# Moving four small steps of a perceiver block's main loop: context sums ahead of the router's shares on GpSimd, logits behind the third quarter's product, choice behind the next norm's moments

## The chip, the cores and the metric

The kernel runs on one core of a Trainium2 chip. The metric is the device time in microseconds (us) of one execution; the figure of a kernel is the median of its timed runs. Engines are called by their names: TensorE (PE in the profile, PEld for its weight loads), VectorE (DVE), ScalarE (ACT), GpSimd (POOL) and SyncE (SP), which issues most of the DMAs.

## The reference, cut to what matters

One block is computed for 16 batches of x (128 tokens x 512 features, float32), each with a context of 2048 x 512:

```
x = x + xattn(layernorm(x), ctx)     # softmax(h ctx^T) ctx, no projections
x = x + attn(layernorm(x))           # 16 heads of 32, rotary on half of each, causal
x = x + ffn(layernorm(x))            # 2 of 8 experts, rank 64
```

The last step is the one whose small parts the change moves. For a batch, the logits are the first token of the normed x times Wr^T (8 x 512). The two largest are kept, their softmax gives two gates, and the residual gets h + sum over both of gate x (h A_e^T) B_e^T:

```
logits = cls_tok @ Wr.T
top_vals, top_idx = jax.lax.top_k(logits, 2)
...
weighted = jnp.einsum('be,belh->blh', gates, expert_out)
return x + weighted
```

## The kernel before, in words

**Stages and order.** All three steps of all batches are in one program, unrolled. The main loop (L1008 to L1122) runs b from 0 to 13. A turn works on several batches at once: b is in its self-attention, l = b - 1 in its expert step, a = b + 1 in its cross-attention product, and s = b + 2 in its cross-attention scores; s + 1 has its first norm prepared. Batches 14 and 15 end in a tail written out by hand (from L1124). There is no planner: the order on every engine is the order of the calls, since each engine is wrapped so that its instructions keep program order (`InOrder`, L95 to L103). An engine therefore executes its list strictly in this order, and an instruction whose input isn't ready holds everything behind it on that engine. All instructions are issued through one helper line, L101, so the profile's rows are told apart by tiles.

**The cross-attention product.** The context of a batch comes in four quarters of 512 rows (`cts[a, v]`), and `attend(a, v, parts)` multiplies the exponentiated scores by quarter v on TensorE. For batches 2 to 14 the products are made with fewer multiplications from sums and differences of halves: `context_halves(a, v)` makes four sums of a context quarter on GpSimd (L344 to L354; tiles `more` and `ctx`), and `token_halves(a)` (L356) makes those of the scores, on VectorE and GpSimd (tile `blocks`). A quarter's product has a first part (8 records in the trace) and a second one (20 records). The first part of quarter 3 reads the last of the four context sums. In the loop the first parts of quarters 0 to 2 come early, then the second parts of 0, 1 and 2 at L1046, L1055 and L1063, and quarter 3 whole at L1078.

**Self-attention of batch b.** `powers(b, g)` (L597) makes a group of four heads: per head a masked scale with a running maximum on VectorE and an exponential on ScalarE. `divided(b, g)` divides a group, on GpSimd for g = 0 to 2, on ScalarE for g = 3. `sums(a)` (L319) adds up the softmax denominators of batch a in one VectorE reduction (tile `part`). `values_begun`, `values_moved`, `values_joined` put the values of b together on VectorE and ScalarE (tiles `vmoved`, `vfirst`, `vv`).

**The router of batch l.** `turn(3, l)` transposes the third norm's rows on VectorE and sends them through DRAM by two SyncE DMAs (`d`, then `hT`). `shares(l)` (L719) multiplies the first token's features by Wr on GpSimd (tile `g_share`), and a VectorE reduction leaves eight partial sums per partition (`g_part`). `logit(l)` (L730) sums these over the partitions with two products by ones on TensorE (`lg`; four records). `choose(l)` (L736) is five VectorE instructions (copy `g_z`, maxima, indices, a cast to `g_at`), one on GpSimd (`g_blocks`) and one on ScalarE. `fetch(l)` gathers the chosen experts' weights with three indirect DMAs from GpSimd (`each` twice, `wb` once) with two small index operations between. `residual(l)` adds the normed rows to x on GpSimd. Later `pair(l)` (L875) copies the gathered `each` on ScalarE for `middle(l)`'s products.

**The next first norm.** `norm1(s + 1)` (L256) is two VectorE instructions (`st`, `mv`) followed by three small ones on GpSimd (`rs` twice, `sh`).

**Space.** The accumulation banks are shared in turn. `logit` takes a bank of the two-deep pool that the scores `psc` use too, and gives it back when `choose` has copied it.

Of the kernel before, what the change touches and what calls it, by code (L numbers as in the profile page):

```python
# [20 lines left out]
B, S, V, D = 16, 128, 2048, 512  # L21
# [45 lines left out]
def perceiver_block(ctx: ExitStack, tc: tile.TileContext, io: dict, out: bass.AP):  # L67
# [38 lines left out]
    def bank(of, tag, name):  # L106
        return of.tile([P, 512], F32, tag=tag, name=name)
# [4 lines left out]
    def early(b):  # L112
        return b < 2

    def late(b):
        return b >= B - 2
# [139 lines left out]
    def norm1(b):  # L256
        norms[1, b] = Norm(xs[b], f"1_{b}", mixed=early(b), hT=(p2, "hT1"), by_act=b > 2).moments()
# [58 lines left out]
    def power(b, v):  # L316
        act.activation(scs[b][:, v], scs[b][:, v], AF.Exp)

    def sums(b, by=dve):  # L319
        sc = scs[b]  # L320
        part = p1.tile([P, S], F32, tag="part", name=f"part_{b}")
        parts[b] = part
        if by_halves(b):
            of = halves_of[b]
            dve.tensor_reduce(
                part.rearrange("p (m t) -> p m t", m=2),
                of[:, :2].rearrange("p m v k t -> p m t (v k)"), AX.X, ALU.add,
            )
            return
        t = p1.tile([P, 4, S], F32, tag="first", name=f"sums_{b}")  # L330
        for v in range(1, VC):
            by.tensor_tensor(t, sc[:, v], t if v > 1 else sc[:, 0], ALU.add)
        by.tensor_tensor(t[:, :2], t[:, :2], t[:, 2:], ALU.add)
        by.tensor_tensor(part, t[:, 0], t[:, 1], ALU.add)
# [6 lines left out]
    def by_halves(b):  # L341
        return 1 < b < B - 1

    def feature_halves(of, more, by=pool):  # L344
        b11, b12, b21, b22 = (of[:, 2 * k : 2 * k + 2, n * HD : (n + 1) * HD] for k in (0, 1) for n in (0, 1))
        by.tensor_tensor(more[:, 1], b22, b12, ALU.subtract)
        by.tensor_tensor(b12, b12, b11, ALU.subtract)
        by.tensor_tensor(more[:, 0], b22, b12, ALU.subtract)
        by.tensor_tensor(more[:, 2], b21, more[:, 0], ALU.subtract)

    def context_halves(b, v):
        if by_halves(b):
            mores[b, v] = p4.tile([P, 3, 2, HD], F32, tag="more", name=f"more_{b}_{v}")
            feature_halves(cts[b, v], mores[b, v])  # L354
# [145 lines left out]
    def order_tokens(b, copy=pool.tensor_copy):  # L500
        hTvs[b] = p1.tile([P, KC, S], F32, tag="hTv", name=f"hTv_{b}")
        copy(
            hTvs[b].rearrange("p c (i b) -> p c i b", i=Q),
            hTs[2, b].rearrange("p i c b -> p c i b"),
        )
# [67 lines left out]
    def values_joined(b):  # L573
        one, two, first, moved = state.pop(("v", b))
        values[b] = p1.tile([P, D], F32, tag="vv", name=f"vv_{b}")
        dve.tensor_tensor(values[b].rearrange("p (n d) -> p n d", n=2), two, first, ALU.add)
# [20 lines left out]
    def powers(b, g):  # L597
        att, nmx, sm, rsm, pss = atts[b]
        hs = slice(4 * g, 4 * g + 4)
        for i in range(hs.start, hs.stop):  # L600

            dve.tensor_tensor_reduce(
                att[:, i, :], pss[g][:, (i - 4 * g) * S : (i - 4 * g + 1) * S],
                cst[:, C_MASK : C_MASK + S], -SCALE, -NEG, ALU.add, ALU.min, nmx[:, i : i + 1],
            )
            act.activation(
                att[:, i, :], att[:, i, :], AF.Exp,
                bias=nmx[:, i : i + 1], scale=-1.0, accum_out=sm[:, i : i + 1],
            )

    def divided(b, g, by=pool):
        att, nmx, sm, rsm, pss = atts[b]
        hs = slice(4 * g, 4 * g + 4)
        dve.reciprocal(rsm[:, hs], sm[:, hs])
        if by is act:
            for i in range(hs.start, hs.stop):
                act.activation(att[:, i, :], att[:, i, :], AF.Copy, scale=rsm[:, i : i + 1])
            return
        by.tensor_tensor(
            att[:, hs, :], att[:, hs, :], rsm[:, hs, None].to_broadcast([P, 4, S]), ALU.mult  # L620
        )
# [92 lines left out]
    def small(b, n, tag, dtype=F32):  # L714
        return p2.tile([P, n], dtype, tag=f"g_{tag}", name=f"g_{tag}_{b}")

    parts_of, logits, chosen = {}, {}, {}

    def shares(b):  # L719
        share, part = small(b, E * KC, "share"), small(b, E, "part")  # L720
        share = share.rearrange("p (e c) -> p e c", e=E)
        first = hTs[3, b][:, 0, :, 0]
        (dve if late(b) else pool).tensor_tensor(
            share, w["r"].rearrange("p c e -> p e c"),
            first[:, None, :].to_broadcast([P, E, KC]), ALU.mult,
        )
        dve.tensor_reduce(part, share, AX.X, ALU.add)
        parts_of[b] = part

    def logit(b):  # L730
        logits[b] = bank(*((ps_acc, "acc") if b >= B - 3 else (ps_sc, "sc")), f"lg_{b}")
        part = parts_of.pop(b)
        for at in (slice(0, P // 2), slice(P // 2, P)):
            matmul(logits[b][at, :E], ones[:, at], part, start=True, stop=True)
# [273 lines left out]
    for b in range(B - 2):  # L1008
        l, a, s = b - 1, b + 1, b + 2
        if b:  # L1010
            order_tokens(b, act.copy)
            value_tokens(b)
            turn_max(a)
            most(a)
            x2_of(l)
        project(b, "q", [0, 1])
        if b:
            spread(a)
            for v in range(VC):
                less(a, v)  # L1020
                power(a, v)
            load_x(s + 1)
        if b:
            rows(3, l)
        project(b, "q", [2, 3])
        rotate(b, "q")
        project(b, "k")
        rotate(b, "k")
        if b:
            turn(3, l)  # L1030
            load_turned(s, 3)
        if b:
            values_by_halves(b)
        else:
            project_v(b)
            keep_v(b)
        rotated(b, "q")
        rotated(b, "k")
        attend(a, 0, (0,))
        attend(a, 1, (0,))  # L1040
        compare(b)
        attend(a, 2, (0,))
        if by_halves(a):
            token_halves(a)
        powers(b, 0)
        attend(a, 0, (1,))  # L1046
        powers(b, 1)
        if b:
            shares(l)
        context_halves(a, 3)  # L1050
        powers(b, 2)
        if b:
            values_begun(b)
        divided(b, 0)
        attend(a, 1, (1,))  # L1055
        powers(b, 3)
        if b:
            values_moved(b)
            logit(l)
        divided(b, 1)  # L1060
        load_ctx(a + 1, 0)
        load_ctx(a + 1, 1)
        attend(a, 2, (1,))  # L1063
        load_ctx(a + 1, 2)
        divided(b, 2)
        if b:
            sums(a)
            values_joined(b)
        divided(b, 3, act)
        if b:  # L1070
            choose(l)
            fetch(l)
            residual(l)
        if s + 1 < B:
            norm1(s + 1)
        if b == 0:
            value_weights()
        attend(a, 3)  # L1078
        load_ctx(a + 1, 3)
        whole(a)  # L1080
        attended(a)
        turn_probs(b, 0)
        if b:
            gate(l)
        begin_join(a)
        turn_probs(b, 1)
        joined(a)
        portion(a)
        x1_of(a)
        score(s, 0)  # L1090
        load_turned(s + 1, 0)
        keep_score(s, 0)
        turn_probs(b, 2)
        if b:
            pair(l)
        rows(2, a)
        score(s, 1)
        load_turned(s + 1, 1)
        keep_score(s, 1)
        turn(2, a)  # L1100
        turn_probs(b, 3)
        if s + 1 < B:
            rows(1, s + 1)
            turn(1, s + 1)
        context_halves(a + 1, 0)
        context_halves(a + 1, 1)
        score(s, 2)
        load_turned(s + 1, 2)
        if b:
            middle(l)  # L1110
        keep_score(s, 2)
        score(s, 3)
        if b:
            heads(b)
            widen(l)
            end(l)
            keep_heads(b)
        else:
            heads_by_halves(b)
        context_halves(a + 1, 2)  # L1120
        keep_score(s, 3)
        join(b)  # L1122

    y, z = B - 2, B - 1  # L1124
    l = y - 1
# [22 lines left out]
    powers(y, 1)  # L1148
    residual(l)
    shares(l)  # L1150
    sums(z, pool)
    powers(y, 2)
    attend(z, 2)
# [70 lines left out]
    end(l)  # L1224
    join_half(z, 0, [0, 1, 2])
    shares(y)
    logit(y)
    join_half(z, 0, [3])
    join_half(z, 1)
# [71 lines left out]
```

## Time and profile before

| what | value |
|---|---|
| median of the 3 timed runs | 769.77 us (768.87 to 770.97) |
| the profiled execution, its own time | 768.3 us |
| its span, first to last instruction | 766.5 us |
| granted TensorE clock over the span | 1.000 |
| TensorE busy | 759.1 us, 99% |
| VectorE busy | 615.0 us, 80% |
| GpSimd busy | 547.5 us, 71% |
| ScalarE busy | 321.5 us, 42% |
| DMA, mean over the span | 237 GB/s |

How to read the lines that follow. A line of the timeline has the start in us from the span's beginning, the duration in us, the engine, the operation with what it writes and reads, how many such in a row it stands for, and in brackets how long the engine was idle before and what ended that. A line of the chain that ended last has a start, a duration, an engine and what it wrote. Busy shares are means over the whole span; matmuls are pipelined, so a start says more than an end. Each turn of the main loop begins, in this text, with the first products of q.

### The profile page before, as it was taken

What the parts mean: (1) busy time and instruction counts of PE and PEld (TensorE: products, weight loads), DVE (VectorE), ACT (ScalarE), POOL (GpSimd) and SP (SyncE); (2) the same over time, 40 slices, a digit from 0 to 9 for tenths busy, and PEclk for the clock granted to TensorE, in tenths of its full rate; (3) what the DMA queues carried; (4) which work ended last, traced back from release to release, by engine and by line L of the source; (5) the groups of instructions that cost most, each with busy time, mean ns of one, the idle gap of its engine ahead of it and who ended that gap; (6) DMA issues with size and microseconds to landing.
All of it is one profiled execution on the core that took longest, in us unless ns stands there. A gap on an engine that the chain in (4) does not pass through costs nothing.

```text
span 766.5 us, 17831 instructions
## 1 busy us (share of the span) xinstructions
PE 759.1 (99%) x6752; PEld 602.3 (79%) x6752; DVE 615.0 (80%) x1678; ACT 321.5 (42%) x947; POOL 547.5 (71%) x604
## 2 busy tenths in 40 slices
PE   9999999999999999999999999999999999999997
PEld 9947587978778797887879788787978868797566
DVE  2447569899898988989899897989989898996466
ACT  1322426335363533535353354535435453442451
POOL 2002577888979888897988888788888979754633
PEclk9999999999999999999999999999999999999999
DMA  9989865759486584947657594765849567461003
GB/s 365 413 308 418 289 234 207 284 182 352 146 307 238 198 312 162 349 164 284 244 210 295 173 343 186 278 235 197 322 151 344 208 250 252 174 233 56 18 13 97
DMA packets 58229, 181.85 MB, mean 237 GB/s; under 512 B 5536, under 2 KB 27696, under 8 KB 41760
## 3 DMA queue, kind: packets, MB, share of 16 engines
q1 hardware_dynamic: 54048, 168.64, 60.0%
q0 software_dynamic: 3952, 12.02, 4.2%
q8 instruction: 53, 0.87, 0.4%
q14 instruction: 32, 0.26, 0.1%
q10 hardware_dynamic: 144, 0.07, 0.0%
HBM read 165.50 MB, written 15.20 MB: 236 GB/s over the span
## 4 chain that ended last, share of the span: by engine, by line
PE 94%; DVE 3%; POOL 1%; ACT 1%; issue 1%; DMA 0%; POOLq 0%
PE psc L101 30%; PE av L101 25%; PE q L101 7%; PE k L101 7%; PE o L101 7%; PE v L101 6%; PE pss L101 2%; PE y L101 2%; PE ffn L101 2%; PE mid L101 2%; PE fill L101 1%; ACT att L101 1%; DVE x L101 1%; PE den L101 1%; POOL more L101 0%
## 5 line engine op out<-in xcount | busy, mean ns | idle before, releaser
L101 PE MATMUL psc<-hT,ctxT 128*128 128x128 f32 x2048 | 233.9, 275 | 0.2 <-ACT hT L101 0.2
L101 PEld LDWEIGHTS psc<-hT,ctxT 128*128 128x128 f32 x2048 | 231.9, 192 | 0.8 <-ACT hT L101 0.4
L101 PE MATMUL av<-ctx,sc 128*64 128x256 f32 (+1 forms) x512 | 144.3, 422 | 0.0
L101 POOL TENSOR_TENSOR more<-ctx 128x512 f32<-128x512 f32 x104 | 132.8, 1277 | 4.4
L101 ACT ACTIVATE att<-att,nmx 128x128 f32<-128x128 f32 x256 | 98.9, 387 | 39.8 <-DVE nmx L101 39.8
L101 PEld LDWEIGHTS av<-ctx,sc 128*64 128x64 f32 (+1 forms) x512 | 72.4, 147 | 46.3 <-issue 19.4
L101 DVE STREAM_TRANSPOSE pT<-att 32x512 f32<-32x512 f32 x140 | 98.2, 701 | 3.8 <-POOL att L101 0.8
L101 PE MATMUL av<-ctx,blocks 128*64 128x256 f32 x416 | 97.1, 380 | 0.0
L101 PE MATMUL av<-more,sc 128*64 128x256 f32 x416 | 82.9, 381 | 0.3 <-POOL more L101 0.3
L101 POOL TENSOR_SCALAR rs<-mv 128x1 f32<-128x1 f32 x48 | 11.1, 232 | 84.2 <-DVE mv L101 82.0
L101 POOL TENSOR_TENSOR more<-ctx,more 128x512 f32<-128x512 f32 x52 | 66.3, 1276 | 4.1
L101 POOL TENSOR_TENSOR ctx<-ctx 128x512 f32<-128x512 f32 x52 | 66.3, 1275 | 4.1
L101 ACT ACTIVATE sc<-sc 128x512 f32<-128x512 f32 x64 | 38.5, 630 | 70.1 <-DVE sc L101 70.1
L101 PEld LDWEIGHTS av<-ctx,blocks 128*64 128x64 f32 x416 | 55.1, 137 | 14.8
L101 PEld LDWEIGHTS q<-hT,w_q 128*128 128x128 f32 x512 | 59.5, 192 | 4.1 <-issue 4.0
L101 PE MATMUL q<-hT,w_q 128*128 128x128 f32 x512 | 61.5, 275 | 0.0
L101 DVE CUSTOM_DVE_ANT_0 att<-pss,cst 128x128 f32<-128x128 f32 x256 | 57.2, 283 | 5.1 <-PE pss L101 4.7
L101 PE MATMUL k<-hT,w_k 128*128 128x128 f32 x512 | 59.8, 275 | 0.0
L101 PEld LDWEIGHTS k<-hT,w_k 128*128 128x128 f32 x512 | 58.5, 192 | 0.0
L101 PE MATMUL o<-w_c,yT 128*128 128x512 f32 (+1 forms) x136 | 58.4, 570 | 0.1
L101 POOL TENSOR_TENSOR att<-att,rsm 128x512 f32<-128x512 f32 x47 | 47.8, 1041 | 12.8 <-DVE rsm L101 12.8
L101 ACT COPY sc<-psc 128x512 f32<-128x512 f32 x64 | 37.2, 581 | 47.0 <-PE psc L101 47.0
(192 smaller groups left out, 1444.2 us busy)
## 6 DMA issues: line engine op xcount, KB each, us to landing
ctxT<-in_ctxT_dram SPq DMA_DIRECT2D x64, 1024.0 KB, 6.7
ctx<-in_ctx_dram SPq DMA_DIRECT2D x64, 1024.0 KB, 7.1
d<-turn SPq DMA_DIRECT2D x42, 256.0 KB, 3.0
hT<-d SPq DMA_DIRECT2D x42, 256.0 KB, 2.8
x<-in_x_dram SPq DMA_DIRECT2D x16, 256.0 KB, 6.1
out_dram<-x POOLq DMA_DIRECT2D x13, 256.0 KB, 6.0
down_q<-in_Wq_downT_dram SPq DMA_DIRECT2D x2, 1024.0 KB, 12.1
down_k<-in_Wk_downT_dram SPq DMA_DIRECT2D x2, 1024.0 KB, 9.9
```

The source lines that it names most:

```text
L101: return lambda *args, **kwargs: tc.keep_in_program_order(issue(*args, **kwargs))
```

## The change

Four calls move within the turn of the loop, and one function is cut in two so that its second half can move by itself.

1. `context_halves(a, 3)` goes in front of `shares(l)` (both have work on GpSimd).
2. `shares` loses its VectorE reduction, which becomes `share_sums`; in the loop that is called behind `sums(a)`. In the tail it directly follows `shares`, as before.
3. `logit(l)` goes from behind `values_moved(b)`, in front of the second part of quarter 2, to behind `values_joined(b)`; on TensorE it then stands between quarter 2's second part and quarter 3.
4. `norm1(s + 1)` goes in front of `choose(l)`, `fetch(l)` and `residual(l)`.

No operation is added or taken away, and no DMA changes its size or queue.

```
@@ shares
+        parts_of[b] = share, part
+
+    def share_sums(b):
+        share, part = parts_of[b]
         dve.tensor_reduce(part, share, AX.X, ALU.add)
         parts_of[b] = part
@@ the loop
         powers(b, 1)
+        context_halves(a, 3)
         if b:
             shares(l)
-        context_halves(a, 3)
         powers(b, 2)
...
             values_moved(b)
-            logit(l)
         divided(b, 1)
...
             sums(a)
+            share_sums(l)
             values_joined(b)
+            logit(l)
         divided(b, 3, act)
+        if s + 1 < B:
+            norm1(s + 1)
         if b:
             choose(l)
             fetch(l)
             residual(l)
-        if s + 1 < B:
-            norm1(s + 1)
@@ the tail, twice
     shares(l)
+    share_sums(l)
```

More of the change, by code (lines that the diff above doesn't have):

```diff
@@ L726, in shares, with share_sums @@
         )
+        parts_of[b] = share, part
+    def share_sums(b):
+        share, part = parts_of[b]
         dve.tensor_reduce(part, share, AX.X, ALU.add)
@@ L1047, in perceiver_block @@
         powers(b, 1)
+        context_halves(a, 3)
         if b:
             shares(l)
-        context_halves(a, 3)
         powers(b, 2)
@@ L1058, in perceiver_block @@
             values_moved(b)
-            logit(l)
         divided(b, 1)
@@ L1067, in perceiver_block @@
             sums(a)
+            share_sums(l)
             values_joined(b)
+            logit(l)
         divided(b, 3, act)
+        if s + 1 < B:
+            norm1(s + 1)
         if b:
@@ L1073, in perceiver_block @@
             residual(l)
-        if s + 1 < B:
-            norm1(s + 1)
         if b == 0:
@@ L1150, in perceiver_block @@
     shares(l)
+    share_sums(l)
     sums(z, pool)
@@ L1226, in perceiver_block @@
     shares(y)
+    share_sums(y)
     logit(y)
```

## The prediction

> **What bounds the kernel now.** I read the page's first part and its chain, then the waits of TensorE, then one steady turn of the main loop, engine by engine, from the timeline.
>
> ```profile
> PE 759.1 (99%) x6752; PEld 602.3 (79%) x6752; DVE 615.0 (80%) x1678; ACT 321.5 (42%) x947; POOL 547.5 (71%) x604
> ...
> PE 94%; DVE 3%; POOL 1%; ACT 1%; issue 1%; DMA 0%; POOLq 0%
> ```
>
> TensorE is busy 99% of the span and carries 94% of the chain that ends last. So nothing that another engine gains is worth anything unless TensorE waits for it, and every wait that TensorE gets is paid in full. The chain in order of time gives the length of a turn, from the first q products of one to those of the next:
>
> ```profile
> 200.32 1.79 PE q L101 x16
> ...
> 246.24 1.79 PE q L101 x16
> ...
> 291.18 1.79 PE q L101 x16
> ```
>
> 246.24 to 291.18 is 44.94 us, and eight of the turns b=2 to 13 take that. Four take more, by the same rows of the chain: b=3 (200.32 to 246.24) 45.92, b=6 45.01, b=9 45.46, b=12 45.35. Together they are 1.98 us above 4 x 44.94. Why is seen in b=3:
>
> ```profile
> 216.30 0.29 POOL L101 TENSOR_TENSOR g_share<-w_r,hT 128x32 f32<-128x32 f32 x1 [2.96 <-DMA hT<-d]
> ...
> 220.62 1.27 POOL L101 TENSOR_TENSOR more<-ctx,more 128x512 f32<-128x512 f32 x1
> ...
> 221.95 0.43 PE L101 MATMUL av<-more,sc 128*64 128x256 f32 x1 [0.34 <-POOL more L101]
> ```
>
> GpSimd stood 2.96 us waiting for the turned norm (hT) that the shares need; the four context operations queued behind the shares came late, and TensorE waited for them. In an ordinary turn (b=4) the same wait is 1.30 us and the last context operation ends at 264.89 + 1.28 = 266.17, before the last quarter's product begins at 266.94 (below).
>
> **Edit 1: context_halves(a, 3) ahead of shares.** Nothing is added. GpSimd's last operation before it ends at 259.26 (257.55 + 1.71, below), so the four operations, 1.35 apart, no longer sit behind the transfer. They end near 265.0 (below), in late turns as well, where they ended at 221.89 with TensorE due some 0.9 us earlier. The stalls of b=3, 6, 9 and 12 go: **-1.98 us**, if nothing is late next. The shares then run at 265.0 to 265.3; in b=4's time scale the latest transfer (b=3) landed at 262.2, so it is covered by 2.8 us.
>
> VectorE and GpSimd do hinder each other here:
>
> ```profile
> 257.55 1.71 POOL L101 TENSOR_TENSOR blocks<-blocks 128x512 f32<-128x512 f32 x1 [0.69 <-DVE blocks L101]
> ...
> 258.05 1.76 DVE L101 TENSOR_TENSOR blocks<-blocks,sc 128x512 f32<-128x512 f32 x1
> ```
>
> VectorE's instruction takes 1.76 where its neighbours of the same size (256.71, 257.44) take 0.70 and 0.69. It ends at 259.81, so it began to work at 259.12, just as GpSimd's 1.71 operation let go. Before, GpSimd then stood idle; now it has a context operation ready. Does that go first? The nearest row: in b=12 a VectorE cast started at 629.18 and took 0.19 (0.17 unhindered) between two of three queued GpSimd multiplications (627.29, 3.05 for three). VectorE got in between. I take no loss for VectorE, and 0.4 us for the first context operation, as the 1.71 row shows (1.28 unhindered): 259.66 + 4 x 1.35 = 265.0. The other end is one whole operation, 1.35 us, on VectorE's path: a rival below.
>
> [...] By "the queue goes first" the sum would be some 17.6 us worse (13 x 1.35); the b=12 cast says no.
>
> **Edit 2: the shares' reduction behind sums(a).** Per turn one 0.17 us VectorE instruction moves. Its old place gave a slot of 0.10 us (261.42 to 261.52 below), so all behind it until sums(a) is 0.10 earlier.
>
> **Edit 3: logit behind the third quarter's product and values_joined.** The products themselves cost the same at either place (0.09 us). But logit needs the reduction, and VectorE reaches that only after sums(a):
>
> ```profile
> 261.42 0.17 DVE L101 TENSOR_REDUCE g_part<-g_share 128x8 f32<-128x32 f32 x1
> ...
> 265.15 1.97 DVE L101 TENSOR_REDUCE part<-blocks 128x128 f32<-128x1024 f32 x1
> ...
> 264.66 0.24 PE L101 MATMUL lg<-g_part,ones 128*64 128x8 f32 x4
> 264.75 0.41 PE L101 MATMUL av<-ctx,sc 128*64 128x256 f32 x1
> ...
> 266.94 0.38 PE L101 MATMUL av<-ctx,sc 128*64 128x256 f32 x1
> ```
>
> The third quarter's second part has 20 records at 0.108: from 264.75 it reaches the last quarter at 266.94. With the 0.09 of lg gone from in front, TensorE comes to logit at 266.85. VectorE: sums end 267.12 - 0.10 = 267.02; an instruction that waits for nothing starts some 0.08 before its forerunner's end (the tail's 746.38 starts 0.09 before 746.28 + 0.19), so 266.94, + 0.17 = 267.11. TensorE reacts 0.05 later (722.15 + 0.76 = 722.91 to its load at 722.96): 267.16. From the load of a logit that had to wait to the next product the tail shows 0.14 (746.77 to 746.91): 267.30 or .31. Before, the last quarter began at 266.94. **The new wait is 0.37 us in each of 13 turns (b=1 to 13): +4.8 us.** TensorE's queue is in order; behind the logit stands the whole last quarter and all after it.
>
> Does VectorE run ahead over time? No: at 253.54 it stood 1.38 us waiting for TensorE's k products, so every turn starts from TensorE, and the distance from k to the reduction is fixed. Bounds: 0.28 (no reaction time, and 0.04 less on VectorE) to 0.65 (the 0.10 slot not gained, and the tail's other logit, which took 0.12 from reduction to load, 751.77 to 751.88, and 0.25 from load to next product). I take 0.37, worked from the nearest rows. The bank that the logit holds longer is next written in score(s, 1), at 273.9; the copy of z at about 269.0 frees it with 4.9 us to spare.
>
> **Edit 4: choose, fetch and residual behind norm1's moments.** On VectorE, two instructions (0.68 + 0.18, 0.86 with their gaps) now stand in front of the choice, whose five end at 269.18 in b=4 and will end near 270.0. On GpSimd the three root operations (0.24, 0.57, 0.26; 275.94 to 277.20 today) go in front of the block numbers, which move from 269.30 to 270.3. Three gathers (each of 1.09, 0.95 and 0.97 to issue), two index operations and the residual follow, all 0.95 later; in turn the roots no longer stand behind them, so GpSimd reaches the next root (277.97, after 0.77 idle) no later. No SP transfer moves. Who waits for the gathers:
>
> ```profile
> 277.51 0.62 ACT L101 COPY paired<-each 128x512 f32<-128x512 f32 x1 [2.87 <-DMA each<-in_A_dram,g_blocks]
> ...
> 279.25 0.81 ACT L101 ACTIVATE h<-x,sh,rs 128x512 f32<-128x512 f32 x1 [1.11 <-POOL sh L101]
> ```
>
> ScalarE's copy waits 2.87 for the gathers, then 1.11 for GpSimd. The 0.95 fits in the 1.11. In the worst turn (b=8, copy at 458.81, 1.48 later within its turn) the operation behind the copy would start some 1.2 later in the turn than in b=4, less the 0.37 that TensorE is late itself; VectorE's maximum behind them (280.56 to 281.25) frees the bank for score 3 at 281.84 with about 0.4 to spare. So nothing in most turns, 0.1 to 0.5 in two or three: **+0.3 us**, with bounds 0 and 0.64 x 12 = 7.7 (a rival).
>
> **Edit 5, the last two batches:** the reduction follows its multiplication as before: 0.
>
> Sum: -1.98 + 4.8 + 0.3 = **+3.1 us**. The profiled execution took 768.3 (span 766.5 and 1.8 around it), so 771.4 for its like; it lies 1.47 under the median of 769.77, to which I add the same: **772.9**.
>
> **Rivals.** (a) *The logit doesn't wait.* If VectorE came to the reduction 0.37 us earlier in the turn, only the gain of edit 1 is left: 769.77 - 1.98 = 767.8; the sum turns negative where the wait falls under 0.13. For it: the 0.10 slot. Against it: sums(a) alone ends 0.17 after TensorE arrives, and it is in front in VectorE's queue. (b) *Late transfers weigh more in the timed runs.* They may be the 1.47 between profile and median; then the gain is 3.45 and the result 771.4, within 0.3%. It decides from about 2.8 us of them. (c) *The gathers become the wait:* they land 0.95 later and another 1.0 for the context loads that they meet, the average copy reaches 33.9 us into the turn where 33.3 is free: 0.64 x 12 = 7.7 more, 780.6. (The twelve copies start on average 32.0 us after the first q record of their turn, 246.08 in b=4; free is 279.25 + 0.37 + 0.4 - 0.62 = 279.40, 33.3 on that scale.) Against it: b=9 issued 0.8 later than b=4 and its copy came 0.3 earlier. (d) *GpSimd goes first at 259.3:* 13 x 1.35 more, 790.5. (e) *The logit waits for more than the reduction* (VectorE's instruction behind it, which carries no signal of its own today, then up to 268.17): about 1.0 x 13 more, 785.9.
>
> **Numbers.** What can be told from no change here is about 0.3%, 2.3 us. Forecast 0.66, (a) 0.06, (b) 0.13, (c) 0.08, (d) 0.05, (e) 0.02. The forecast's own range is 771.4 (13 x 0.28 - 1.98 more) to 775.5 (13 x 0.55 - 1.98 + 0.6 more); about a tenth of it lies under 772.1. So slower 0.74 (0.59 of the forecast, c, d, e), same 0.23 (0.07 of it, b, half of a), faster 0.03 (the other half of a; the timed runs spread by 2.1). The range reaches down to (b) less 0.6 for the spread of the runs, and up to a wait of 0.65 with 1.8 from the gathers (8.4 - 1.98 + 1.8): 770.8 to 778.0; (a), (d), (e) and most of (c) are left out.
>
> **What would show it.** TensorE's waits list lg behind VectorE's g_part, 13 times, some 0.3 to 0.4 each; turns of 45.3 with no long ones among them; no wait of av for more. Right for edit 1: GpSimd's more at 259.3, g_share with no wait for hT. Right for edit 4: each issued 0.9 later, paired later, score 3 unmoved. Wrong: no wait of lg (a), token halves above 1.76 on VectorE (d), turns above 45.8 with psc waiting (c).

## The result, and the profile after

| | kernel before | changed kernel |
|---|---|---|
| median of 13 runs each | 770.25 us (768.78 to 772.37) | 772.31 us (771.84 to 774.11) |
| the profiled execution, its own time | 768.3 | 771.89 |
| its span | 766.5 | 769.9 |
| turns b=1 to 13, first q record to first q record | 586.40 | 589.87 |

The ratio is 1.0028, with a 95% interval of 1.0018 to 1.0039: slower by 2.1 us (1.4 to 3.0), so the sign is sure, and whether it is over the 0.3% that the prediction counts as no change isn't. The prediction was 772.9, +3.1.

The profile's line of busy times (engine, us, share of the span, instructions) and the shares of its chain, which answer to the first two lines shown of before:

```profile
PE 760.4 (99%) x6752; PEld 599.1 (78%) x6752; DVE 611.0 (79%) x1678; ACT 321.0 (42%) x947; POOL 553.7 (72%) x604
...
PE 71%; DVE 21%; issue 5%; ACT 1%; POOL 0%; DVEq 0%; POOLq 0%
```

The shares of busy time hardly moved, and TensorE is at 99% again. The chain tells what the shares don't: 21% of it now runs over VectorE, where it was 3%. In every turn something that TensorE needs ends last on VectorE. The list of waits names it (load side of TensorE; total us, times, longest):

```profile
PEld lg L101 <- DVE g_part L101: 8.4, 13, 0.7
...
PEld psc L101 <- DVE mx L101: 0.2, 1, 0.2
```

Thirteen waits of the logit for the reduction. The 8.4 us overstate the loss, because the logit's weight load begins 0.21 before its product where it doesn't wait (264.45 and 264.66 for b=4 in the kernel before) and this lead counts as waiting too (for b=4 the load is listed with 0.64); the turns below show what is lost. No wait of av for more is left. The timeline of b=4 (start, length, engine, operation, and in brackets what the instruction waited for), rows of VectorE, then TensorE, then GpSimd:

```profile
258.31 1.76 DVE L101 TENSOR_TENSOR blocks<-blocks,sc 128x512 f32<-128x512 f32 x1
...
265.31 1.97 DVE L101 TENSOR_REDUCE part<-blocks 128x128 f32<-128x1024 f32 x1
267.18 0.20 DVE L101 TENSOR_REDUCE g_part<-g_share 128x8 f32<-128x32 f32 x1
...
266.64 0.60 PE L101 MATMUL av<-more,sc 128*64 128x256 f32 x4
267.43 0.29 PE L101 MATMUL lg<-g_part,ones 128*64 128x8 f32 x4 [0.19 <-DVE g_part L101]
267.57 0.41 PE L101 MATMUL av<-ctx,sc 128*64 128x256 f32 x1
...
259.48 1.73 POOL L101 TENSOR_TENSOR more<-ctx 128x512 f32<-128x512 f32 x1
...
264.01 1.28 POOL L101 TENSOR_TENSOR more<-ctx,more 128x512 f32<-128x512 f32 x1
265.25 0.30 POOL L101 TENSOR_TENSOR g_share<-w_r,hT 128x32 f32<-128x32 f32 x1
```

Read the GpSimd rows first: the context sums end at 265.29 and the shares follow at once, with no idle time in brackets, since their transfer had landed by then. VectorE begins the reduction only when sums(a) is done. TensorE has issued its last product of the third quarter at about 266.85 and starts the logit at 267.43, 0.05 after the reduction's end. And the turns, from the chain in order of time (start, length, the first q products of each turn):

```profile
201.15 1.79 PE q L101 x16
...
246.50 1.79 PE q L101 x16
...
291.84 1.79 PE q L101 x16
```

Turn b=3 shrank from 45.92 to 45.35, and b=4 grew from 44.94 to 45.34: the long turns are gone, and all turns but b=1 (45.65) have the same new length.

### The profile page after: what moved, and what is told of

Its sections match the earlier page's. It is cut to its first block, busy times and chain, and to the rows that moved or that the text cites. A ratio compares the mean times of both kernels' runs of the same rounds, so it can differ in the third digit from the quotient of the medians.

```text
span 769.9 us, 17832 instructions
## 1 busy us (share of the span) xinstructions
PE 760.4 (99%) x6752; PEld 599.1 (78%) x6752; DVE 611.0 (79%) x1678; ACT 321.0 (42%) x947; POOL 553.7 (72%) x604
## 4 chain that ended last, share of the span: by engine, by line
PE 71%; DVE 21%; issue 5%; ACT 1%; POOL 0%; DVEq 0%; POOLq 0%
PE psc L101 30%; PE av L101 11%; PE k L101 7%; PE q L101 7%; PE o L101 6%; DVE att L101 6%; DVE blocks L101 4%; PE y L101 2%; PE ffn L101 2%; PE mid L101 2%; DVE kP L101 1%; DVE v L101 1%; DVE vmoved L101 1%; DVE sc L101 1%; DVE kT L101 1%
## 5 line engine op out<-in xcount | busy, mean ns | idle before, releaser
L101 POOL TENSOR_TENSOR more<-ctx 128x512 f32<-128x512 f32 x104 | 138.7, 1334 | 4.4
L101 PEld LDWEIGHTS av<-ctx,blocks 128*64 128x64 f32 x416 | 57.0, 137 | 15.0
```

The lines of the kernel that those rows point to most:

```text
L101: return lambda *args, **kwargs: tc.keep_in_program_order(issue(*args, **kwargs))
```

## The experiments

My theory after the result: the time is the old length of the ordinary turns plus a wait of 0.41 in each, minus the long turns, which the earlier context sums removed. Rivals: that the later choice and gathers cost it; that GpSimd's earlier work hinders VectorE; and, on the other side, that the context sums are a gain by themselves whatever the rest does. All ratios are to the kernel before, run on the same chip.

| run | median us | ratio, 95% interval |
|---|---|---|
| changed kernel | 772.31 | 1.0028 (1.0018 to 1.0039) |
| e1 reduction first | 766.32 | 0.9954 (0.994 to 0.9967) |
| e2 logit 0.87 us later | 766.55 | 0.9953 (0.994 to 0.9967) |
| e3 reduction twice | 775.04 | 1.0065 (1.0051 to 1.0079) |
| e4 without part 4 | 771.88 | 1.0017 (1.0006 to 1.0029) |
| e5 without part 1 | 774.18 | 1.0046 (1.0032 to 1.006) |
| e6 part 1 alone | 805.98 | 1.0463 (1.0447 to 1.0479) |
| e7 part 4 alone | 771.37 | 1.001 (0.9994 to 1.0026) |
| e8 e1, gathers later | 771.74 | 1.0016 (1.0003 to 1.003) |
| e9 e1 without part 4 | 766.46 | 0.9947 (0.9934 to 0.9961) |
| e10 before again | 770.69 | 1.0001 (0.9991 to 1.001) |

**e1: the reduction in front of sums(a).**

```
         divided(b, 2)
         if b:
-            sums(a)
             share_sums(l)
+            sums(a)
             values_joined(b)
             logit(l)
```

> The changed kernel, with the reduction of the shares in front of sums(a) instead of behind it; the logit stays where the change put it. Theory (TensorE's new wait is VectorE's sums plus the reduction): the reduction ends some 1.7 us earlier, the logit waits for nothing, turns are 44.94 and the long turns stay away, so 2 us under the kernel before by its profile (about 768), and 3.5 to 4 under it if the timed runs lose more to late transfers than the profile does. Rival 1 (later choice and gathers are the cost): still slower than before, by 1 to 3 us. Rival 2 (GpSimd's earlier context sums hinder VectorE): turns stay at 45.3.

Measured: 766.32, 3.6 under the kernel before and 6 under the changed one. Its VectorE and TensorE rows for b=4:

```profile
264.32 0.19 DVE L101 TENSOR_REDUCE g_part<-g_share 128x8 f32<-128x32 f32 x1 [0.17 <-POOL g_share L101]
264.43 2.00 DVE L101 TENSOR_REDUCE part<-blocks 128x128 f32<-128x1024 f32 x1
...
265.83 0.24 PE L101 MATMUL lg<-g_part,ones 128*64 128x8 f32 x4
265.92 0.41 PE L101 MATMUL av<-ctx,sc 128*64 128x256 f32 x1
```

The reduction ends 1.3 us before the logit is due; VectorE pays 0.17 of waiting for the shares, which nobody misses. The logit has no bracket, and all turns b=1 to 13 are 44.94. The fourth part and GpSimd's earlier sums are still in this kernel, so neither can be the cost of 0.41 in each turn: both rivals fall.

**e2: the logit later on TensorE.**

```
             values_joined(b)
+            attend(a, 3, (0,))
             logit(l)
...
-        attend(a, 3)
+        attend(a, 3, (1,) if b else (0, 1))
```

> The changed kernel, with the logit between the first and the second part of the last quarter, that is 8 product records (0.87 us) later on TensorE; VectorE's order is that of the change. Theory: the wait was 0.41 us, less than 0.87, so it goes and the time is that of the kernel with the reduction first, within 0.5 us. Rival (the loss is on VectorE or GpSimd, not where TensorE meets the logit): as slow as the changed kernel.

Measured: 766.55. The same wait is removed from the other end: VectorE is as late as in the changed kernel, and TensorE has 0.87 us of other products first. Two edits on different engines with one result leave the meeting point of the two as the only place of the loss. Turns b=2 and 3 of its profile were 45.13 and 44.97, all others 44.94; b=2 is told under e8.

**e3: the wait made longer.**

```
         share, part = parts_of[b]
+        if 0 < b + 1 < B - 2:
+            dve.tensor_reduce(part, share, AX.X, ALU.add)
         dve.tensor_reduce(part, share, AX.X, ALU.add)
```

> The changed kernel, with the reduction of the shares made twice in a row in the loop's 13 turns (same input, same output). Theory: VectorE's path to the logit is longer by one instruction, 0.10 to 0.17 us, and TensorE pays it in full: 13 x 0.10 to 0.17 = 1.3 to 2.2 us over the changed kernel, turns of 45.45 to 45.52. Rival (the wait has another cause, or there is slack): no difference from the changed kernel.

Measured: 1.0065 against 1.0028, so 2.8 us over the changed kernel, more than the 1.3 to 2.2 expected. The two reductions show as

```profile
268.65 0.40 DVE L101 TENSOR_REDUCE g_part<-g_share 128x8 f32<-128x32 f32 x2
```

so the second costs 0.20, not 0.10 to 0.17 (it writes the same tile as the first; whether that is why wasn't tested), and turns are 45.57, 0.22 longer, but for b=1 (46.38), where TensorE also waited 0.6 for another VectorE result. 13 x 0.22 = 2.9. TensorE pays in full for what VectorE adds, and only the size of the added piece was misjudged.

**e4 and e7: the fourth part, taken away and by itself.** The edit of e4, on the changed kernel:

```
-        if s + 1 < B:
-            norm1(s + 1)
         if b:
             choose(l)
             fetch(l)
             residual(l)
+        if s + 1 < B:
+            norm1(s + 1)
```

e7 is the kernel before with the reverse of these lines as its only edit.

> The changed kernel without its fourth part: choose, fetch and residual in front of the next norm's moments, as before the change. Theory: the gathers are hidden in all turns but b=1, so at most 0.3 us faster than the changed kernel, which 5 rounds may not tell from none; turns stay at 45.35. Rival (the later gathers cost more than the profile's one turn shows): 1 us or more faster.

> The kernel before, with its fourth part alone: the next norm's moments in front of choose, fetch and residual. Theory: the gathers are issued some 0.9 us later and nothing on TensorE notices: within 1 us of the kernel before, long turns as before. Rival (later gathers reach TensorE through ScalarE's copy): 2 us or more slower, with waits of psc or mid in several turns.

Measured: e4 1.0017 where the changed kernel has 1.0028; the intervals overlap, so some 0.8 us by the ratios, which isn't told from none. e7 1.001, with an interval that includes 1. The times alone exclude neither the rival of e4 (1 us) nor the expected 0.3. The profiles speak against both rivals: the 13 turns of e4 are together only 0.2 shorter than those of the changed kernel (589.69 and 589.87), and e7 has no wait of psc for VectorE's mx and none of mid for the copy. e7 keeps the long turns of the kernel before (b=3, 6, 9 and 12).

**e5: without the first part** (shares in front of context_halves again, the rest as changed).

> The changed kernel without its first part: the shares in front of context_halves(a, 3) on GpSimd, as before; reduction, logit and choice where the change put them. Theory: all 13 turns keep the logit's wait (45.35), and turns whose transfer is late get, on top, only what GpSimd's last context sum is later than the waiting logit: about 0.5 in a turn such as b=3 of the profile before (last sum at 21.74 of the turn, last quarter at 21.24), none in mild ones. So 0.5 to 2 us over the changed kernel, with a wait of av for more in a few turns. Rival (moving the context sums is worth the whole 2 us or more by itself): 2 us or more over it.

Measured: 774.18, ratio 1.0046 against 1.0028, some 1.4 us over the changed kernel. The waits of its profile:

```profile
PEld lg L101 <- DVE g_part L101: 8.3, 13, 0.7
...
PEld av L101 <- POOL more L101: 2.7, 3, 1.2
...
PEld psc L101 <- DVE mx L101: 0.8, 1, 0.8
```

The logit's waits are unchanged, and in three turns (b=6, 9 and 12) the wait for the context sums comes on top. That the waiting logit partly covers what is late anyway would make the first part worth less beside the new wait (1.4) than the 3.6 that e1 gains. That isn't shown: the intervals of e5 and of the changed kernel overlap, and the execution profiled here, the slowest of six (776.33), has 4.2 more in its 13 turns than the changed kernel (594.06 and 589.87).

**e6: the first part alone**, on the kernel before.

> The kernel before, with its first part alone: context_halves(a, 3) in front of shares(l); reduction, logit and choice as before. Theory: VectorE's reduction in its old place, at 15.3 of the turn, now waits until GpSimd has made the shares, at 19.2, and two groups of powers stand behind it; the logit in its old place (18.6) waits some 0.8 to 1.0 on TensorE. At least 13 x 0.8 - 2 = 8 us slower than the kernel before, and up to 13 x 3 more where VectorE can't make up its 3.9 us within a turn. Rival (early context sums are a gain whatever the rest does): 2 us or more faster.

Measured: 805.98, 35 us slower; turns are 47.95. The reduction in its old place, in front of two groups of powers, and the waits of TensorE:

```profile
273.04 0.19 DVE L101 TENSOR_REDUCE g_part<-g_share 128x8 f32<-128x32 f32 x1 [3.80 <-POOL g_share L101]
```

```profile
PEld psc L101 <- DVE mx L101: 23.1, 13, 1.9
...
PEld lg L101 <- DVE g_part L101: 15.1, 13, 1.2
...
PEld den L101 <- DVE part L101: 5.9, 13, 0.5
```

VectorE stands 3.8 us for the shares, and TensorE meets that delay twice in a turn, at the logit and at the bank of the scores: counted from the turn's first q record, the logit of b=4 starts at 19.46 where it started at 18.58 before, and score 3 at 38.66 where it started at 35.76. The wait of den is no third place: the kernel before has 5.6 of it too, put down to several releasers. The second part isn't a refinement of the first but its condition.

**e8: the gathers later still**, on e1.

```
             choose(l)
-            fetch(l)
             residual(l)
+            fetch(l)
```

> The kernel of the first experiment (reduction first), with residual(l) in front of fetch(l): the three gathers are issued another 1.28 us later, nothing is added. This measures how far ScalarE's copy follows the issue. If the gathers' landing is set by their issue, copies come 1.28 later, at 33.0 of the turn on average, and several turns lose 0.2 to 1 us: 3 to 8 us over the first experiment (766.3). If it is set by the context loads that they share the DMA engines with, copies come less than 0.5 later and it costs under 1 us.

Measured: 771.74, 5.4 over e1, within the first branch. This run shows the edge that part 4 moves towards. In b=2 ScalarE, and TensorE's products:

```profile
188.53 0.62 ACT L101 COPY paired<-each 128x512 f32<-128x512 f32 x1 [5.07 <-DMA each<-in_A_dram,g_blocks]
```

```profile
189.76 1.06 PE L101 MATMUL mid<-hT,paired 128*128 128x128 f32 x8
191.11 1.16 PE L101 MATMUL psc<-hT,ctxT 128*128 128x128 f32 x8 [0.29 <-DVE mx L101]
```

```profile
PEld psc L101 <- DVE mx L101: 3.4, 7, 0.7
```

The copy waits 5.07 for the gathers, VectorE's maximum behind it comes late, and score 3 waits for its bank. Seven turns have that wait, and seven are long. For nine turns of this one profile, the copy's start after the turn's first q record against the turn's length:

| b | 1 | 3 | 6 | 9 | 5 | 2 | 4 | 12 | 10 |
|---|---|---|---|---|---|---|---|---|---|
| copy starts at | 33.07 | 32.19 | 31.64 | 33.31 | 33.50 | 33.63 | 33.64 | 33.80 | 33.87 |
| turn | 44.94 | 44.94 | 44.94 | 45.18 | 45.37 | 45.50 | 45.51 | 45.67 | 45.74 |

Past 33.07 the turn is longer by just what the copy is later (33.63 - 33.07 = 0.56, 45.50 - 44.94 = 0.56); the four turns left out of the table fit too (b=11: 33.64 and 45.51; the others start earlier and take 44.94). With the logit's wait the edge moves with TensorE to 33.07 + 0.41 = 33.48, and so it fits the changed kernel: its b=1 has the copy at 33.78 and is 0.30 longer than the rest, its b=8 at 33.38 and is not. It fits e4 as well, which lacks part 4: its b=5 has the copy at 33.63 and is 0.15 longer. Turn b=2 of e2 (33.26) lost 0.19 in the same way.

**e9: e1 without the fourth part.**

> The kernel of the first experiment (reduction first), with choose, fetch and residual in front of the next norm's moments, as before the change. Theory: the logit waits for nothing and the gathers have some 1 us more room; as fast as the first experiment (766.3), at most 0.5 us faster in the median, with a smaller spread. Rival (the fourth part helps by itself): slower than the first experiment.

Measured: 766.46 and 0.9947, against 766.32 and 0.9954 of e1: no difference that could be told from none. Its turns are 44.94 but for b=1 (45.21), which the copy (at 32.50) doesn't explain. These two and e2 are faster than both kernels, by 3.4 to 4.2 us against before.

**e10: the kernel before, profiled again.**

> The kernel before, unchanged, profiled a second time, to see whether the loss to late transfers is the same in every execution. Theory (its timed runs lie 1.5 to 2 us over the profile used for the prediction because more transfers are late in them): the number of long turns and their sum over 44.94 differ from the first profile's 1.98, and the time of this execution differs by the same amount. Rival: the same four long turns with the same 1.98, whatever the time.

Measured: this profiled execution took 770.45, 2.15 more than the one the prediction was worked from, with the same kernel. Its turn b=6, from the chain:

```profile
335.99 1.79 PE q L101 x16
...
345.39 4.04 DMA d<-turn
349.48 2.67 DMA hT<-d
352.51 1.25 POOL more L101
...
382.17 1.79 PE q L101 x16
```

46.18, where the first profile had 45.01: the first of the two transfers took 4.04, so the second began only at 349.48, and GpSimd's context sums followed it. The first profile shows the same place of the delay. Its SyncE queue in b=3, and then in b=4:

```profile
209.72 0.33 SPq L101 DMA_DIRECT2D d<-turn  x1
213.41 0.38 SPq L101 DMA_DIRECT2D hT<-d  x1
...
255.64 0.33 SPq L101 DMA_DIRECT2D d<-turn  x1
257.69 0.38 SPq L101 DMA_DIRECT2D hT<-d  x1
```

Both turns issue d at the same place (9.57 and 9.56 of the turn), and hT, which waits for it, follows 3.69 later in the long turn and 2.05 later in the ordinary one. The four long turns are the same ones (b=3, 6, 9, 12), contrary to the part of my theory that their number varies; but together they are 4.25 over 4 x 44.94 instead of 1.98. The difference, 2.27, is close to that of the two times, 2.15. So the loss that part 1 removes is 2 to 4 us in these two executions, and differs from execution to execution. Why d is late in every third turn stays open.

## Right or wrong, step by step

**Edit 1, -1.98:** right as a mechanism, and small for a usual execution (1.98 in the one of 768.3, 4.25 in that of 770.45; the median of the kernel before is 770.25). The long turns vanished with it (45.35 after, but for b=1, and 44.94 throughout in e1). That VectorE would get in ahead of GpSimd's queue was right: its third token operation takes 1.75 or 1.76 in all 13 turns, as before, and GpSimd's first context operation 1.72 or 1.73 where it took 1.27 to 1.29 before, the 0.4 that I allowed. The prediction had a single row for it. In b=4 VectorE's operation started at 258.31, ahead of GpSimd's at 259.48. Rival (d) fell.

**Edit 2, 0.10 earlier:** right; sums(a) ends at 20.95 of the turn where it ended at 21.04.

**Edit 3, +0.37 a turn:** right, 0.41 measured (45.35 - 44.94). The instant at which the last quarter would start was 21.22 to 21.23 after the turn's first q record by my sum, and is 21.24; the reduction took 0.20 instead of 0.17. It is in all 13 turns, so it doesn't drift, as VectorE starts each turn from TensorE's products (in the changed kernel it stands 0.87 for those of k in b=1, and 1.43 to 1.45 in the others). Rivals (a) and (e) fell: the wait is there, and it is for the reduction alone. The pause between TensorE's starts is 0.6 (about 266.85 to 267.43 in b=4), and the granted clock stayed at 1.000 over the span.

**Edit 4, +0.3:** the profile has 0.30 in b=1 and nothing elsewhere, so the size agrees, but in part by luck: which copy comes late differs between executions. e4, without part 4, lost 0.15 in this way, and e1, with it, nothing; the times don't show the term. The edge was right: the prediction put it at 33.3 of the turn, and e8 makes it 33.48 beside the logit's wait. The working was partly wrong. I let the copies land 0.95 later because they are issued that much later. e9 and e1 differ by 1.05 in the issue of the gathers (23.71 and 24.76 of the turn) and by nothing in the average copy of turns 1 to 12 (31.71 and 31.72); e4 and the changed kernel differ by as much in the issue and by 0.27 in the copy (32.03 and 32.30), which is no more than the 0.25 between e1 and e2 (31.97), whose gathers are issued at the same place. The next 1.11 (e8, 25.87) moves the copy by 1.35, to 33.08. So by these single profiles something other than the issue sets when the gathers are there up to an issue at about 24.8, and after that their own issue does. That this something is the context loads is my guess, not shown. Rival (c) was real but one step away.

**The sum, +3.1:** the profile's own difference is +3.4 (769.9 - 766.5; 3.47 in the 13 turns), which is 13 x 0.41 + 0.3 - 1.98 = 3.65 less the 0.19 by which b=1 was already long before. The measured difference of medians is smaller, +2.06. The step that failed is the last one, "it lies 1.47 under the median of 769.77, to which I add the same". The distance between profile and median was not a constant: it was the part of the loss to late transfers that this profile happened not to have, as e10 shows, and part 1 removes that too. The changed kernel, whose profile has no such loss, has its median only 0.4 above its profiled run. Rival (b) named this and was given 0.13; it was half true, and the result lies between it (771.4 by its sum) and the forecast. That 772.9 comes within 0.6 of the measured 772.31, while the difference is a whole microsecond off, is partly luck: the kernel before came out at 770.25 over 13 runs, 0.48 above the three runs that the forecast started from.

## What to carry to other kernels

Where one engine is busy throughout, a small step that it takes from another engine belongs where its input has been ready for a while, and that is decided in the other engine's queue as much as in its own: with 1.97 us of other VectorE work in front of a 0.20 us reduction the kernel was 2.1 us slower, and with the two lines swapped it was some 3.6 us faster. Before a difference is carried from one profile to a median, look whether the profile's own excess turns are a loss that the change removes; if so, profile twice.

## What the runs showed of the hardware that I had not expected

In these profiles the use of the gathered data did not follow the gathers' issue until a certain point: 1.05 us earlier or later moved the average copy by 0.01 in one pair of kernels and by 0.27 in another, the next 1.11 us by 1.35. And beyond the edge of 33.07 us TensorE's turn of this kernel grows by the lateness of one ScalarE copy (0.56 for 0.56 in e8), through a VectorE maximum and a score bank, with no smoothing. Where GpSimd had a further operation queued and VectorE's was waiting, VectorE's went in between in all 13 turns (1.75 or 1.76 us each, as in the kernel before).
